# A four-layer graph network on one core: the fallback branch put last, layer 0's update set around the last far sums, and the products d and s in slot tiles of their own

## The chip, the core and the metric

The kernel runs on one core of a Trainium2 chip, in one launch. The metric is device microseconds of the whole program. All times are in microseconds (us) unless another unit is named.

The core has five engines that work side by side, each in the order of its own queue: TensorE (PE; its weight loads are listed as PEld), VectorE (DVE), ScalarE (ACT), GpSimd (POOL) and SyncE (SP), which here only issues transfers. They wait for each other by semaphores. SBUF is the working memory; PSUM holds what TensorE writes, in banks of 512 f32 per partition.

## What is computed

2708 nodes with 128 features `x`, and a dense matrix `adj` in which some 2.4% of the entries are not zero (with weights). Four layers follow each other, each as `x = layernorm(x + layer(x, adj))`. The change touches layer 0 and the way the layers hang together:

```python
s = x @ msg_w[:, :128].T
d = x @ msg_w[:, 128:].T
messages = gelu(s[:, None, :] + d[None, :, :] + msg_b)     # one vector for each pair i, j
aggregated = einsum('ijd,ij->id', messages, adj)
h = gelu(concat([x, aggregated]) @ upd_w.T + upd_b) + x
x = layernorm(x + layernorm(h) * ln_w + ln_b)
```

Layer 1 is a gated attention: queries and keys from `x`, `sigmoid(q k^T)` times `adj` twice, a product with the messages, an update and a layernorm. Layer 2 is a hyperbolic attention over the same pairs. Layer 3 is two products with `adj`, each followed by a matrix and a swish. Layers 1 to 3 keep their computation and their order.

## The kernel before

**Tiles.** The nodes are taken in NT = 22 tiles of 128 (the last has 20 rows), as columns in NB = 22 blocks of JB = 124, and as rows i of layer 0 in LT = 22 tiles of LR = 125 (NC = 5 groups of RG = 25). `groups()` gives the tiles of an update in seven groups: five of four tiles, one of one, and the last with 20 rows. `runs()` gives two halves of 11 tiles.

**Layer 0** computes the gelu only for pairs with an edge. In a block (one row tile by one column block) TensorE picks, for each row and each column of the block, the slots of the first few edges: ten matmuls `pick` (L716) of a selection S with `dA`, which holds d and the adjacency, each as two f16 parts (hi and lo) whose sum is the f32 value, once for each of the five groups; then L721 adds s. ScalarE takes the gelu of the slots (L760), VectorE weighs them (L747), and TensorE adds them up (L732, `add_up`). Edges beyond the slots of a block are "far": VectorE takes the largest of them by weight for each row (up to 16, in two rounds of 8), L676 finds their place, SP loads the row's s into `far` (`start_far`, far<-s_tab), POOL fetches and adds the rows of d with eight indirect transfers (L680), ScalarE takes their gelu (L686), and VectorE sums them (L694). `turn` and `close` (L700 to L706) add far and near sums and put them, transposed, into `aggT`. The three slot tiles `sl_all` (two PSUM banks each) are used in turn by the blocks.

The order of layer 0 is written out by hand (`tc.manual_schedule()`): every step has a block number at which it is issued (`when()`, `preparation()`), and the loop over the 484 blocks issues block by block the pick, the gelu, the weighing of the block before, and the steps that are due. Steps of the last rows with a number above 484 are issued after the loop.

**The preparation** is the part of these steps with negative numbers. `turn_x` transposes x on TensorE (L423) into the slot tiles, two groups of four tiles in the two banks of a tile, and DVE or ACT copies (L425). Then six `Piece`s of four tiles each come. `products` computes d (L449) in bank 0 of a slot tile and s (L460) in bank 1 of the same tile; DVE copies d (L453), ACT writes the hi part five times, once for a group (L455, 2560 elements), DVE adds the bias to s (L462), ACT takes s's hi part (L464), SP stores both to DRAM tables. `update` computes `x @ upd_w[:128] + upd_b` into u_tab (L478, L480). `rests` gives the lo parts on DVE (L488, L490), and POOL copies d's lo part to the four other groups (L492). Between these steps lie the first rows' own: masks (L579), ranks (L587, L588, L628), edges past the slots (L638 to L645), adjacency parts.

**After the loop** the count of rows that the sparse way cannot do, `bad_n`, is summed (L777 to L785: six small VectorE operations, one matmul, one cast), then the far steps of the last row tile are issued. SP loads u_tab into `new` (L791). All engines load `bad_n` (L793) and compare (L794): if it is above 0, layer 0 is done densely (it is 0 for these inputs, so the branch jumps over it). Then the update: for each group the product of `aggT` (L851) is added to `new` (L852), a gelu, x is added (L854), moments (L173). POOL computes `xb = x + ln_b` for all tiles in one instruction (L846). `resnorm` does two layernorms by halves: first half add, second half add, first half end, second half end. A layernorm's small values are chains of short VectorE operations with a square root on ScalarE; its scaling is one operation for a tile, on VectorE (L194) and ScalarE (L192) together.

**Layer 1** starts with transposes of two weights (L880, copied at L882) and of x (L892), and gives messages, keys and queries by groups (L895 to L899). POOL adds the bias row to x (L901) and then loads three broadcast vectors for layer 2 (`y_vecs`, L264); VectorE multiplies them at L270. SP loads rows of `adjT` ahead, three for layer 1 (L911) and four for layer 2 (L1122).

Of the kernel before, what the change touches and what calls it, by code (L numbers as in the profile page):

```python
# [11 lines left out]
F32 = mybir.dt.float32  # L12
BF16 = mybir.dt.bfloat16
# [6 lines left out]
P = 128  # L20
# [18 lines left out]
def gnn_stack(ctx: ExitStack, tc: tile.TileContext, t, out: bass.AP):  # L39
# [13 lines left out]

    def weight(name, k0=0):
        w = const.tile([P, D], F32, name=f"w_{name}_{k0}")
        nc.sync.dma_start(out=w, in_=t[name][k0:k0 + P, :])
        return w

    def column(name):
        c = const.tile([P, 1], F32, name=f"col_{name}")  # L60
        nc.sync.dma_start(out=c, in_=t[name].rearrange("(p o) -> p o", o=1))
        return c

    def across(name):
        n = t[name].shape[0]
        r = const.tile([P, n], F32, name=f"row_{name}")
        nc.gpsimd.dma_start(out=r, in_=t[name].partition_broadcast(P))
        return r
# [4 lines left out]
    nc.vector.memset(x[:, NT - 1, :], 0.0)  # L73
    if NFULL:
        nc.sync.dma_start(out=x[:, :NFULL, :], in_=t["x"][:NFULL * P, :].rearrange("(n p) d -> p n d", p=P))
    if NFULL < NT:
        nc.sync.dma_start(out=x[:rows[-1], NT - 1, :], in_=t["x"][NFULL * P:, :])
# [14 lines left out]
    class Values:  # L92
# [5 lines left out]
        def new(self, like=None):  # L98
            self.n += 1
            shape = [P, NT] if like is None else list(like.shape)  # L100
            return self.pool.tile(shape, F32, name=f"{self.tag}{self.n}")

# [93 lines left out]
    def resnorm(h, xb, g, st, V, sq=None):  # L196

        st2 = V.pool.tile([P, NT, 6], F32, name=f"{V.tag}_st2")
        for a, b in runs():
            normalize(h, h, st, a, b, V)  # L200
            nc.vector.tensor_tensor(h[:, a:b, :], h[:, a:b, :], over_tiles(g, b - a), op=ALU.mult)
            nc.vector.tensor_tensor(x[:, a:b, :], xb[:, a:b, :], h[:, a:b, :], op=ALU.add)
            moments(st2, x, a, b)
        for a, b in runs():
            normalize(x, x, st2, a, b, V, sq)
# [119 lines left out]
    with ExitStack() as l0:  # L325
# [6 lines left out]
        bad_n = wp.tile([1, 1], mybir.dt.int32, name="bad_n")  # L332
# [4 lines left out]
        with ExitStack() as msg:  # L337
# [80 lines left out]
            def turn_x():  # L418
                for n, (a, b) in enumerate(spans(0, NT, 4)):
                    ps = sl_all[n // 2][:, n % 2, :]  # L420
# [6 lines left out]
            class Piece:  # L427
# [7 lines left out]
                def products(self):  # L435
                    b0, b1, a0, a1 = self.b0, self.b1, self.a0, self.a1
                    ps = sl_all[(self.n + 1) % 3].rearrange("p k (b d) -> p k b d", d=D)
# [9 lines left out]
                    for b in range(b0, b1):  # L447
                        r = min(JB, N - b * JB)
                        nc.tensor.matmul(ps[:r, 0, b - b0, :], xT[:, b * JB:b * JB + r], msg_d, start=True, stop=True)  # L449
                        if r < JB:  # L450
                            nc.vector.tensor_copy(d[:r, b - b0, :], ps[:r, 0, b - b0, :])
                    full = min(b1, NFB) - b0
                    nc.vector.tensor_copy(d[:, :full, :], ps[:JB, 0, :full, :])  # L453
                    self.hi, self.lo = (v[:, b0:b1, :, :D] for v in dA)
                    nc.scalar.activation(self.hi, d[:, :, None, :].to_broadcast([JB, b1 - b0, NC, D]), AF.Copy,  # L455
                                         scale=D_SCALE)
                    for a, b, r in groups():
                        if a0 <= a < a1:
                            for i in range(a, b):
                                nc.tensor.matmul(ps[:r, 1, i - a0, :], xT[:, i * P:i * P + r], msg_s,  # L460
                                                 start=True, stop=True)
                            nc.vector.tensor_tensor(s[:r, a - a0:b - a0, :], ps[:r, 1, a - a0:b - a0, :],  # L462
# [4 lines left out]
                    for p0, p1 in even(JB):  # L467
                        nc.sync.dma_start(out=rows_of_d[p0:p1, b0:b1, :], in_=d[p0:p1])

# [15 lines left out]
                def rests(self):  # L485
# [6 lines left out]
                    nc.gpsimd.tensor_copy(lo[:, :, 1:, :], lo[:, :, 0:1, :].to_broadcast([JB, b1 - b0, NC - 1, D]))  # L492
# [12 lines left out]
            class Rows:  # L505
# [125 lines left out]
                def past(self, m):  # L631
                    if m == 0:
                        self.o = op_.tile([P, NB, JB], F32, name="o")
# [105 lines left out]

            LAG = 3  # L740
            assert NC == 5 and NB % 2 == 0
            R = [Rows(i) for i in range(LT)]
            steps = sorted(((g, n, step) for n, (g, step) in enumerate(x for v in [preparation(), *(v.when() for v in R)] for x in v)),
                           key=lambda x: x[:2])
            with tc.manual_schedule():
# [27 lines left out]

                most = vp.tile([P, 1], F32, name="most")
# [12 lines left out]
                for _, _, step in steps:  # L787
                    step()

        new = l0.enter_context(tc.tile_pool(name="l0x", bufs=1, reuse_waits="tile")).tile([P, NT, D], F32, name="new")  # L790
        nc.sync.dma_start(out=new, in_=u_tab.rearrange("(n p) d -> p n d", p=P))  # L791

        n_bad = nc.values_load(bad_n[0:1, 0:1])  # L793
        with tc.If(n_bad > 0), ExitStack() as msg:  # L794
            mp = msg.enter_context(tc.tile_pool(name="all", bufs=1))
            ap_ = msg.enter_context(tc.tile_pool(name="adjrows", bufs=2))
            gp = msg.enter_context(tc.tile_pool(name="gelu", bufs=3))
            psum = msg.enter_context(tc.tile_pool(name="ps_l0", bufs=2, space=PSUM))
            pbc = msg.enter_context(tc.tile_pool(name="ps_bc", bufs=2, space=PSUM))

            sel = mp.tile([3 * RG, RG], BF16, name="sel")
            nc.vector.tensor_add(sel, ident[:3 * RG, 0:RG], ident[:3 * RG, RG:2 * RG])
            nc.vector.tensor_add(sel, sel, ident[:3 * RG, 2 * RG:3 * RG])

            xT = mp.tile([P, N], F32, name="xT")
            sT = mp.tile([P, N], F32, name="sT")
            dT = mp.tile([P, N], F32, name="dT")
            transposed(xT, x, psum)  # L810
            linear_T(sT, msg_s, xT, psum, bias=msg_b)
            linear_T(dT, msg_d, xT, psum)

            HALF_N = -(-N // 2)
            halves = spans(0, N, HALF_N)
            part = mp.tile([P, N, len(halves)], F32, name="part")
            for g0 in range(0, N, RG):
                r0 = min(g0, N - RG)
                a = ap_.tile([3 * RG, N], F32, name="a")
                for k in range(3):  # L820
                    nc.sync.dma_start(out=a[k * RG:(k + 1) * RG, :], in_=adj[r0:r0 + RG, :])
                s = ap_.tile([3 * RG, N], BF16, name="s")
                nc.gpsimd.tensor_copy(s, a)
                for n in (2 * RG, RG):
                    nc.gpsimd.tensor_tensor(a[:n, :], a[:n, :], s[:n, :], op=ALU.subtract)
                    nc.gpsimd.tensor_copy(s[:n, :], a[:n, :])
                for i in range(g0, min(g0 + RG, N)):
                    one = sel[:, i - r0:i - r0 + 1].to_broadcast([3 * RG, P])
                    g = gp.tile([P, N], F32, name="g")
                    nc.scalar.activation(g, dT, AF.Gelu, bias=sT[:, i:i + 1])  # L830
                    for h, (b0, b1) in enumerate(halves):
                        bc = pbc.tile([P, HALF_N], F32, name="bc")
                        for c0, c1 in spans(b0, b1, BANK):
                            nc.tensor.matmul(bc[:, c0 - b0:c1 - b0], one, s[:, c0:c1], start=True, stop=True)
                        nc.vector.scalar_tensor_tensor(
                            g[:, b0:b1], g[:, b0:b1], 1.0, bc[:, :b1 - b0], op0=ALU.mult, op1=ALU.mult,
                            accum_out=part[:, i, h:h + 1])
            nc.vector.tensor_add(aggT[:, :N], part[:, :, 0], part[:, :, 1])

        with ExitStack() as upd:  # L840
            rp = upd.enter_context(tc.tile_pool(name="upd", bufs=1))
            psum = upd.enter_context(tc.tile_pool(name="ps_upd", bufs=4, space=PSUM))
            V = Values(rp, "v0_")
            xb = rp.tile([P, NT, D], F32, name="xb")
            st = rp.tile([P, NT, 6], F32, name="st")
            nc.gpsimd.tensor_tensor(xb, x, over_tiles(ln_b), op=ALU.add)  # L846
            for a, b, r in groups():
                g = new[:r, a:b, :]
                ps = psum.tile([P, BANK // D, D], F32, name="ps")
                for i in range(a, b):  # L850
                    nc.tensor.matmul(ps[:r, i - a, :], aggT[:, i * P:i * P + r], upd_a, start=True, stop=True)  # L851
                nc.vector.tensor_tensor(g, g, ps[:r, :b - a, :], op=ALU.add)  # L852
                nc.scalar.activation(g, g, AF.Gelu)
                nc.vector.tensor_tensor(g, g, x[:r, a:b, :], op=ALU.add)  # L854
                moments(st, new, a, b)
            resnorm(new, xb, ln_w, st, V)


# [663 lines left out]
```

## Time and profile before

| | |
|---|---|
| median of 3 runs | 2005.69 (2005.01 to 2007.13) |
| profiled execution | 2005.42 |
| its span | 2003.7 (1.7 lie around it) |
| mean granted TensorE clock | 0.918 |
| busy: PE, DVE, ACT, POOL | 1675.0, 1517.8, 1105.9, 666.0 |
| first pick (L716) | at 67.04 |
| last add-up of layer 0 ends | at 894.2 |
| x of layer 0 finished | at 953.54 |
| last output write issued, end of span | 2000.25, 2003.7 |

A line of the timeline has the start, the length, the engine, the line and operation, what is written and read, and in brackets how long the engine had been idle before and what released it. SPq, DVEq and ACTq are the sequencers of the engines: transfers issued, branches and register loads. A line of waits has who waited for whom, the sum, how often and the longest.

### The profile page before, as it was taken

What the parts mean: (1) busy time and instruction counts of PE and PEld (TensorE: products, weight loads), DVE (VectorE), ACT (ScalarE), POOL (GpSimd) and SP (SyncE); (2) the same over time, 40 slices, a digit from 0 to 9 for tenths busy, and PEclk for the clock granted to TensorE, in tenths of its full rate; (3) what the DMA queues carried; (4) which work ended last, traced back from release to release, by engine and by line L of the source; (5) the groups of instructions that cost most, each with busy time, mean ns of one, the idle gap of its engine ahead of it and who ended that gap; (6) DMA issues with size and microseconds to landing.
All of it is one profiled execution on the core that took longest, in us unless ns stands there. A gap on an engine that the chain in (4) does not pass through costs nothing. (4 is left out here: it accounts for less than half of the span.)

```text
span 2003.7 us, 36396 instructions
## 1 busy us (share of the span) xinstructions
PE 1675.0 (84%) x14037; PEld 959.1 (48%) x14037; DVE 1517.8 (76%) x3507; ACT 1105.9 (55%) x1510; POOL 666.0 (33%) x417
## 2 busy tenths in 40 slices
PE   5799999999999999871899994689999974079996
PEld 5566666666666666651444433423222322034543
DVE  5899999999999999857556567889999997820105
ACT  3567667666666676642333331599998993300103
POOL 2467767757767667461100000012000350000000
PEclk8899999999999999995899996779998987579998
DMA  7666666666667666343133310022222215135230
GB/s 178 155 139 131 133 136 140 126 136 148 124 133 148 130 129 139 73 85 143 36 135 136 142 60 0 1 87 87 75 80 94 80 42 245 46 115 187 107 127 28
DMA packets 218358, 222.25 MB, mean 111 GB/s; under 512 B 28372, under 2 KB 204474, under 8 KB 211714
## 3 DMA queue, kind: packets, MB, share of 16 engines
q1 hardware_dynamic: 167038, 195.95, 32.2%
q0 software_dynamic: 51136, 23.88, 10.3%
q8 instruction: 112, 1.84, 0.4%
q14 instruction: 72, 0.59, 0.1%
HBM read 211.94 MB, written 7.83 MB: 110 GB/s over the span
## 5 line engine op out<-in xcount | busy, mean ns | idle before, releaser
L680 POOL DMA_INDIRECT far<-d_tab,ix x352 | 563.0, 1599 | 257.5 <-DVE W L747 110.7
L760 ACT ACTIVATE g<-sl 128x768 f32<-128x768 f32 x484 | 393.0, 812 | 255.9 <-PE sl L721 199.1
L716 PE MATMUL sl<-dA,S 124*128 124x153 f16 x4840 | 408.0, 231 | 10.1 <-DVE W L747 7.7
L716 PEld LDWEIGHTS <-S 124*128 124x128 f16 x4840 | 330.4, 98 | 79.7 <-issue 67.9
L732 PE MATMUL acc<-g,W 128*32 128x128 f32 x4840 | 205.5, 277 | 0.7 <-DVE ones L777 0.7
L1125 POOL TENSOR_TENSOR at<-at,off 128x128 f32<-128x128 f32 (+1 forms) x22 | 68.1, 3113 | 338.1 <-DMA at<-in_adjT 320.4
L1441 PE MATMUL acc<-held,x 128*128 128x512 f32 (+1 forms) x240 | 99.6, 563 | 84.0 <-DVE x L194 84.0
L732 PEld LDWEIGHTS acc<-g,W 128*32 128x32 f32 x4840 | 140.6, 109 | 58.9 <-issue 54.7
L721 PE MATMUL sl<-s,same 50*128 50x384 f16 x968 | 161.9, 308 | 0.0
L233 DVE TENSOR_TENSOR g<-ps,row_L_gnn_b 128x512 f32<-128x512 f32 (+2 forms) x14 | 7.9, 572 | 197.1 <-PE ps L231 197.0
L923 ACT ACTIVATE w<-lg,row_L_gnn_gate_bias 128x512 f32<-128x512 f32 (+1 forms) x132 | 80.7, 634 | 137.8 <-PE lg L922 74.3
L1181 PE MATMUL accV<-m,X 128*128 128x512 f32 (+4 forms) x264 | 128.4, 628 | 33.6 <-DVE m L1171 29.2
L747 DVE TENSOR_TENSOR W<-sl,own 128x150 f32<-128x150 f32 x484 | 143.0, 299 | 14.6 <-ACT g L760 14.1
L1133 PE MATMUL ps<-XT 128*128 128x512 f32 (+4 forms) x264 | 143.2, 626 | 3.1 <-ACT m L1138 2.8
L676 DVE FIND_INDEX8 ix<-v,o 128x8 uint32<-128x2728 f32 x44 | 131.7, 2993 | 0.0
L607 DVE TENSOR_SCALAR S<-rk 124x1000 f16<-124x1000 bf16 (+1 forms) x330 | 129.4, 418 | 0.0
L922 PE MATMUL lg<-qT,mT 128*128 128x512 f32 (+2 forms) x264 | 115.5, 567 | 13.5 <-ACT w L923 9.9
L925 DVE TENSOR_TENSOR w<-w,at 128x2708 f32<-128x2708 f32 (+1 forms) x22 | 65.4, 2974 | 79.3 <-ACT w L923 79.3
L694 DVE SCALAR_TENSOR_TENSOR extra<-far,v,extra 128x128 f32<-128x128 f32 x330 | 114.4, 347 | 12.3 <-ACT far L686 6.0
L1441 PE MATMUL acc<-at,x 128*128 128x512 f32 (+3 forms) x288 | 116.7, 552 | 0.0
L638 DVE SCALAR_TENSOR_TENSOR o<-ps,ar 128x496 f32<-128x496 f32 x132 | 82.4, 624 | 38.3 <-issue 22.6
L1400 ACT COPY nT<-acc 128x512 f32<-128x512 f32 (+1 forms) x12 | 6.4, 530 | 186.7 <-PE acc L1441 186.7
(310 smaller groups left out, 2687.1 us busy)
## 6 DMA issues: line engine op xcount, KB each, us to landing
at<-in_adjT SPq DMA_DIRECT2D x40, 1354.0 KB
ar<-in_adj SPq DMA_DIRECT2D x105, 248.0 KB
far<-s_tab SPq DMA_DIRECT2D x44, 512.0 KB
at<-in_adjT SPq DMA_DIRECT2D x42, 448.0 KB
at<-in_adjT SPq DMA_DIRECT2D x21, 704.0 KB
at<-in_adjT SPq DMA_DIRECT2D x21, 650.0 KB
held<-in_adjT SPq DMA_DIRECT2D x10, 1354.0 KB
at<-in_adjT SPq DMA_DIRECT2D x21, 280.0 KB
```

The source lines that it names most:

```text
L607: nc.vector.tensor_scalar(self.S[h][:, :n, :, k * RG:(k + 1) * RG], self.rk[h][:, :n, :LR].rearrange("p b (c i) -> p b c i", c=NC), EDGE + ...
L676: nc.vector.max_index(ix, self.v[:, n * 8:n * 8 + 8], self.o.rearrange("p b j -> p (b j)"))
L680: nc.gpsimd.indirect_dma_start(out=self.far[n][:, k, :], out_offset=None, in_=d_tab[:, :], in_offset=bass.IndirectOffsetOnAxis(ap=self.ix[ ...
L716: nc.tensor.matmul(group[c], self.S[h][:, n, c, :], dA[q][:, b, c, :], start=c % 3 == 0 and q == 0, stop=False)
L721: nc.tensor.matmul(out, same[p], self.s3[p, :e - a, :], start=False, stop=True)
L732: nc.tensor.matmul(self.acc[q:q + 32, k, :], W[:, c, :], g[:, c, :], start=b == 0 and k == 0, stop=ends)
L747: nc.vector.tensor_tensor(W[:, :, :RG].rearrange("p (k c) i -> p k c i", k=2), columns_of(sl, D, DA), own[:, None, None, :].to_broadcast([ ...
L760: nc.scalar.activation(g.rearrange("p (k c) d -> p k c d", k=2), columns_of(sl, 0, D), AF.Gelu, scale=1.0 / D_SCALE)
L922: nc.tensor.matmul(lg[:r, :b - a], mT[:, j * P:j * P + r], qT[:, a:b], start=True, stop=True)
L1133: nc.tensor.matmul(ps, XT[:, self.js], XT[:, c], start=True, stop=False)
L1181: nc.tensor.matmul(accV[:, a:b], X[:self.r, self.j, :], self.m[:, a:b], start=first, stop=last)
L1441: nc.tensor.matmul(acc[k], src[:rows[j], j, :], at[:rows[j], a:b], start=j == order[0], stop=j == order[-1])
```

## The change

Three things are changed.

*The branch.* `n_bad` is read and compared at the end of the whole kernel and no longer between the sums and the update of layer 0. Layers 1 to 3 become a function. If `n_bad` is above 0, x is loaded again, layer 0 is done densely with its own update, and layers 1 to 3 are run once more. To the program that adds a second copy of these layers that is not run. The weights' loads are cached, so that the second copy uses the same tiles.

*The update.* It moves into the hand-written order. u_tab is loaded as a step of the last row tile, into the buffer `o` in which the edges past the slots were searched, and so ahead of the last load of far<-s_tab. The update of the first five groups (20 tiles, whose sums are closed before) is issued around the last far gelu and the last far sums; the half of the first 11 tiles is added next, then come groups 5 and 6, the other half, and the two ends. `ln_b` is added to x in place, a group at a time, on POOL. Small values lie in slots of the `g` pool, products in the slot tiles. The check of bad rows (seven operations, as before) comes behind all this.

*The pieces.* d and s get bank 0 of two different slot tiles. The copy of d is ACT's. ACT writes d's hi part once (512 elements) and POOL spreads it to the four other groups, as it did for the lo part. `turn_x` takes the slot tiles in the order 0, 1, 2.

```diff
             def turn_x():
-                    ps = sl_all[n // 2][:, n % 2, :]
+                    ps = sl_all[n % 3][:, n // 3, :]
...
                 def products(self):
-                    ps = sl_all[(self.n + 1) % 3].rearrange("p k (b d) -> p k b d", d=D)
+                    psd, pss = (sl_all[(2 * self.n + k) % 3][:, 0, :].rearrange("p (b d) -> p b d", d=D)
+                                for k in range(2))
...
-                    nc.vector.tensor_copy(d[:, :full, :], ps[:JB, 0, :full, :])
+                    nc.scalar.copy(d[:, :full, :], psd[:JB, :full, :])
...
-                    nc.scalar.activation(self.hi, d[:, :, None, :].to_broadcast([JB, b1 - b0, NC, D]), AF.Copy,
-                                         scale=D_SCALE)
+                    nc.scalar.activation(self.hi[:, :, 0, :], d, AF.Copy, scale=D_SCALE)
+                    self.spread(self.hi)
...
+                def spread(self, v):
+                    nc.gpsimd.tensor_copy(v[:, :, 1:, :], v[:, :, 0:1, :].to_broadcast(
+                        [JB, self.b1 - self.b0, NC - 1, D]))
...
+            class Update:
+                def when(self):
+                    yield (LT - 1) * NB + 7, self.load
+                def load(self):
+                    o = op_.tile([P, max(NB * JB, NT * D)], F32, name="o")
+                    self.new = o[:, :NT * D].rearrange("p (n d) -> p n d", d=D)
+                    nc.sync.dma_start(out=self.new, in_=u_tab.rearrange("(n p) d -> p n d", p=P))
...
+                def sums(self, n):
+                    a, b, r = groups()[n]
+                    g, ps = self.new[:r, a:b, :], sl_all[n % 3][:r, n // 3 % 2, :].rearrange("p (i d) -> p i d", d=D)
+                    for i in range(a, b):
+                        nc.tensor.matmul(ps[:, i - a, :], aggT[:, i * P:i * P + r], upd_a, start=True, stop=True)
+                    nc.vector.tensor_tensor(g, g, ps[:, :b - a, :], op=ALU.add)
+                    nc.scalar.activation(g, g, AF.Gelu)
+                def rows(self, n):
+                    a, b, r = groups()[n]
+                    g = self.new[:r, a:b, :]
+                    nc.vector.tensor_tensor(g, g, x[:r, a:b, :], op=ALU.add)
+                    moments(self.st, self.new, a, b)
+                    nc.gpsimd.tensor_tensor(x[:r, a:b, :], x[:r, a:b, :], over_tiles(ln_b, b - a, r), op=ALU.add)
...
                 R[-1].add_up(late)
+                rest = [step for _, _, step in steps]
+                last_gelu, far_sums, last_turn = rest[0], rest[1:9], rest[9:]
+                G = len(groups())
+                ahead = LR * (LT - 1) // BANK
+                U.open()
+                for n in range(ahead):
+                    U.sums(n)
+                    if n > 0:
+                        U.rows(n - 1)
+                    if n == 1:
+                        last_gelu()
+                    if n == 2:
+                        for step in far_sums:
+                            step()
+                for step in last_turn:
+                    step()
+                U.rows(ahead - 1)
+                early, late = runs()
+                U.norm.add(*early)
+                for n in range(ahead, G):
+                    U.sums(n)
+                for n in range(ahead, G):
+                    U.rows(n)
+                U.norm.add(*late)
+                U.norm.end(*early)
+                U.norm.end(*late)
...
-                for _, _, step in steps:
-                    step()
...
+    with ExitStack() as top:
+        layers_1_to_3(top)
+    n_bad = nc.values_load(bad_n[0:1, 0:1])
+    with tc.If(n_bad > 0), ExitStack() as top:
+        load_x()
+        all_pairs()
+        layers_1_to_3(top)
```

## What is predicted

> **What bounds the kernel now.** I began with engines by stretch. The first row is the preparation of layer 0 (from the end of the transposes of x to the first pick, L716), the second its 484 blocks, the third all from the last add-up to the finished x. The columns are length, busy time and instructions of each engine, granted clock, DMA share, GB/s.
>
> ```profile
> core 0: us, PE busy (x) PEld busy (x) DVE busy (x) ACT busy (x) POOL busy (x), PEclk, DMA share, GB/s
> 18.30:67.00 48.70, 31.07 (x157) 27.03 (x157) 31.35 (x67) 21.64 (x21) 10.51 (x5) 0.77 0.72 179
> 67.00:894.20 827.20, 781.50 (x11368) 561.00 (x11366) 761.26 (x2170) 554.11 (x823) 563.99 (x353) 1.00 0.63 128
> 894.20:953.70 59.50, 10.15 (x54) 9.21 (x54) 38.86 (x158) 13.44 (x32) 6.14 (x2) 0.59 0.40 146
> ```
>
> The loop is TensorE's: 94% busy, 1.71 us a block. The change does not touch it, so what the stretches around it gain or lose is the result. Both are chains of waits: no engine is busy for more than two thirds of either. Next the waits of the preparation (who waited for whom, us in total, times, longest):
>
> ```profile
> POOL dA L492 <- DVE dA L490: 42.1, 5, 15.1
> ACT dA L455 <- DVE g L453: 21.9, 6, 6.6
> PE sl L460 <- DVE g L453: 11.6, 6, 3.6
> PE sl L423 <- DVE aggT L425: 2.4, 3, 0.8
> ```
>
> PE loses 11.6 us before the s products, because VectorE's copy of d reads the tile they write, and 2.4 us in the transposes. POOL is idle for most of the stretch. The timeline shows one such piece and the neighbour of a POOL copy:
>
> ```profile
> 36.42 0.68 DVE L453 COPY g<-sl 124x512 f32<-124x512 f32 x1
> 37.14 2.35 ACT L455 ACTIVATE dA<-g 124x2560 f16<-124x2560 f32 x1 [4.58 <-DVE g L453]
> 37.16 2.08 PE L460 MATMUL sl<-w_L_msg_wT,aggT 128*128 128x128 f32 x8 [1.18 <-DVE g L453]
> ...
> 51.94 2.03 POOL L492 COPY dA<-dA 124x2048 f16<-124x2048 f16 x1 [5.68 <-DVE dA L490]
> 53.48 0.91 DVE L579 TENSOR_SCALAR mask<-at 124x768 bf16<-124x768 f32 x1
> ```
>
> Last the timeline behind the loop, down to layer 1's first query copy:
>
> ```profile
> 892.13 0.71 SPq L791 DMA_DIRECT2D new<-u_tab  x1
> ...
> 901.37 1.06 ACT L686 ACTIVATE far<-far 128x1024 f32<-128x1024 f32 x1 [6.52 <-issue]
> 902.46 3.06 DVE L694 SCALAR_TENSOR_TENSOR extra<-far,v,extra 128x128 f32<-128x128 f32 x8 [6.02 <-ACT far L686]
> ...
> 907.50 0.26 ACT L706 COPY aggT<-ps 128x125 f32<-128x125 f32 x1 [5.08 <-PE ps L703]
> 910.71 0.29 PEld L851 LDWEIGHTS ps<-w_L_upd_wT,aggT 128*128 128x128 f32 x1 [3.38 <-ACTq L794]
> 910.73 3.01 SPq L911 DMA_DIRECT2D at<-in_adjT  x3
> ```
> ```profile
> 965.02 0.56 DVE L270 TENSOR_TENSOR y_prods<-y_vecs 128x384 f32<-128x384 f32 x1 [3.76 <-DMA y_vecs<-in_L_gnn_att_wr]
> 965.50 0.68 DVE L899 COPY qT<-ps_q 128x512 f32<-128x512 f32 x1
> ```
>
> VectorE does nothing useful from 894 to 902.5 while the last fetched rows land, then all wait for the turn and the branch (16 us from 894.2 to 910.7), and only then does the update start, although 20 of 22 tiles' sums were closed long before. At the end VectorE stands 3.76 us at L270 for y_vecs, ahead of the query copy that layer 1 waits for.
>
> **Preparation: −8 us, between −11 and −4.** Own banks for d and s take away the 11.6 us; three transposed groups that need no copy first take 2.4: at most 14.0 on PE. VectorE loses L453, 6 × 0.68 + 0.5 = 4.6 us. ScalarE takes these copies (7, about 0.6 each, +3.7) and its L455 falls from 2.35 to 0.63 (a 512-element copy, as L464): 6 × −1.72 = −10.3. I walked the list in order, each instruction starting when its engine and its producers are free, at the trace's durations: PE leaves the transposes at 16.1 instead of 18.3, and the first pick comes at 57.6 instead of 67.04, −9.4. The other 4.6 of the 14.0 come back as waits for the ranks' chain (L588, L640), to which PE now comes sooner. The same bytes (48.7 us × 179 GB/s = 8.7 MB) in 39.3 us are 222 GB/s, a share of 0.89: not yet full on average, but 24.6 to 34 us is at 0.99 already, so an engine may wait for a load there. Against it stand six new POOL copies like L492 (2.0 us, the last 1.05), 11 us in POOL's idle time; the last is due only when block 20 is picked. If that cover were gone, the next piece would come up to 2 us late.
>
> What they cost VectorE is open. By the row, L579's mask of 768 took 0.91 us beside L492 and 0.54 at 846.7 with no copy beside it: 0.37 an overlap, some four of six on VectorE's path, 1.5 us. The Trainium skill ("SBUF — State Buffer", Who interferes with whom) has a harder rule, against this change: VectorE and GpSimd share a port pair as an exclusive lock, and the loser stands for the whole instruction: up to 11 us. The row shows a slow-down of a third of a microsecond, no stand of 2, so I take 1.5: −9.4 + 1.5 = −7.9. Ends: −11 (more than the walk, if the ranks' waits do not all return) and −4 (nearly three full stands of 2).
>
> **Layer 0's end: x finished 9.3 us sooner, −5 at layer 1, between −9.3 and −1.3.** In the old clock: the last add-up ends at 894.2, the first group's sum at 895.5. Five groups at 2.34 (L852 0.69, residual 0.67, statistics 0.87 and a gap) and 3.2 of far sums are 14.9: VectorE is through at 910.7. Then the early half's add: value chain 4.0 with its Sqrt table load of 1.28, 2.2 for the scaling (8 × 0.27), 1.62 twice, statistics 2.22: 922.4. Groups 5 and 6 add 2: 924.5. The late half's add 10.2, the two ends 4.8 and 4.6: 944.2, against 953.54. The far sums, the turn and the 2.6 us of branch now lie beside VectorE's other work; the old 6.12 us row addition on POOL (L846) becomes seven pieces under the same cover. The second table load (Gelu back, 1.28) is hidden by VectorE's queue.
>
> Two orders are moved on SP. The u_tab load goes from 892.1 to where the `o` tile comes free (the last FIND_INDEX8, L676, ends at 867.6) and stands ahead of the last far<-s_tab load. It takes DMA 8 us by its old landing, the s_tab load about 4: 880, and POOL needs that at 879.7: 0 to 2 us, inside the 6.5 us that the last gelu waited. In return, it no longer delays the last fetch. Second, layer 1's first loads (L911) waited for nothing after 910.7; now their tile is free only after the check of the bad rows, which stands behind the update (six small operations and a cast, 1.7 us, before hidden at 895): 945.4. They and the four of layer 2 are 7.0 MB and took 17 us at 400 GB/s and more, so they end about 963.7.
>
> That is where the gain is cut. Layer 1's transposes start 6.1 us earlier (948.6 for 954.76; the check and the transposes of its weights come between), and the first query product is there at 956. But ahead of its copy VectorE waits at L270. POOL issues y_vecs behind its own 6.13 us addition, at 950.6 to 952.3. In the trace they landed 3.3 us later with DMA empty: 955.6, and the gain stays 9.3. Now they land among the 7.0 MB. The nearest row is the start: a broadcast row issued at 2.36 beside the load of x landed at 10.70, 8.3 later. The Trainium skill ("DMA: Bandwidth & Descriptors", Queues, rings and completion order) says an engine goes round its queues packet by packet, which would put y_vecs ahead of most of the 7.0 MB: some 955.6 to 958. The row, with its 8.3, gives 960. I take the row, as it holds the same kind of transfer beside the same kind of load: the copy moves from 965.5 to about 960.5, −5. The bounds are 9.3 (no contention) and 1.3 (they end with the loads at 963.7).
>
> **Branch at the end: +1.7, between +0.8 and +4.** The load of the count (0.48) and the branch stand behind everything. ScalarE's took 2.6 us (908.0 to 910.6), VectorE's 2.9, POOL's 4.3 beside a full DMA. The last output write is issued at 2000.3 and lands at 2002.8, 2.5 us that hide most of it on the engines that are done at 2000.0: 0.5 + 2.9 − 2.5 = 0.9, and if SP branches only after its write, 3.4. I take 1.7. Without the cover it is 3.4.
>
> Sum, against the profiled execution (2005.42, its span 2003.7 and 1.7 around it): −7.9 − 5 + 1.7 = −11.2, so 1994.2; that execution is 0.3 below the median of 2005.69, the same by any measure here.
>
> **Rivals.** *The preparation's gain is eaten by DMA*: its stretch is at 0.99 from 24.6 to 34 and a shorter one asks for more; then only turn_x's 2 us stay, −2 − 5 + 1.7 = −5.3: 2000. For it: the share; against it: PE's waits name VectorE, not DMA. *y_vecs end with the loads*: −7.9 − 1.3 + 1.7 = −7.5: 1998. *y_vecs pass them*: −7.9 − 9.3 + 1.7 = −15.5: 1990. *The port lock, slower*: each of the twelve POOL copies of the preparation holds VectorE for its whole 2 us, the six new ones on the path of the piece. They cost 11 us plus what the earlier pieces now run into; that decides from 9.4 + 5 − 1.7 = 12.7 us, 2.1 a copy. With 2.7 a copy and the branch at +4, the time is 2005.4 − 9.4 − 5 + 16 + 4 = 2011. The 0.91 of L579 speaks against it. *It does not overlap as it says*: the update's second gelu stands behind the last far gelu on ScalarE in order, and if the fetch lands as late as 901.4, VectorE stops until then: the start is lost by up to 5 us, and the time is 1998, not more, as nothing else of the update waits for it.
>
> **Chances.** Forecast (1991 to 1997.5) 0.45; y_vecs pass or the walk is exceeded (1985 to 1991) 0.18; y_vecs with the loads, the late gelu or DMA in the preparation (1997.5 to 2001.7) 0.23; several of them together, no change to be told 0.09; the lock, slower 0.05. A measurement of this kernel tells about 0.2%, 4 us, from none: faster 0.86, same 0.09, slower 0.05. The range is 1986 to 2001.5.
>
> **What would show it.** First pick at 57 to 61; no PE wait for a copy at the s products; operations of VectorE beside POOL copies longer by about 0.4, not 2; the last far gelu before 899 less the shift; x finished about 17 before its old 953.5; a wait of some 4 us at the y_vecs products with the first loads of layer 1 in flight; behind the last output write 1 to 2 us of branch. The forecast is wrong if the first pick stays near 65, if layer 1 begins less than 10 us sooner, or if the loop's 827 us change.

## The result, and the profile after

The changed kernel takes 1994.97 us (median of 5 runs, 1993.64 to 1996.88) against 2005.84 of the kernel before in the same session: ratio 0.9943, 95% interval 0.9933 to 0.9954. The forecast was 1994.2. The number was met; two of its three terms were not, and it was luck that their errors cancel. The profiled executions show it, stage by stage (1993.64 with a span of 1991.8, against 2005.42 and 2003.7):

| stage, by its marks in the two traces | before | after | difference | forecast |
|---|---|---|---|---|
| start to first pick | 67.04 | 53.08 | −14.0 | −7.9 |
| first pick to the last add-up's end | 827.15 | 827.46 | +0.3 | 0 |
| from there to x of layer 0 | 59.35 | 49.82 | −9.5 | −9.3 |
| from x to the first query copy | 11.96 | 17.55 | +5.6 | +4.3 |
| from there to the issue of the last output write | 1034.75 | 1035.16 | +0.4 | 0 |
| from there to the end of the span | 3.45 | 8.73 | +5.3 | +1.7 |
| sum | 2003.7 | 1991.8 | −11.9 | −11.2 |

Engines by stretch after the change, in the columns of the prediction's first fence: preparation (from the end of the transposes), loop, update.

```profile
core 0: us, PE busy (x) PEld busy (x) DVE busy (x) ACT busy (x) POOL busy (x), PEclk, DMA share, GB/s
14.50:53.08 38.58, 22.48 (x157) 19.59 (x157) 34.14 (x61) 16.04 (x30) 20.66 (x11) 0.84 0.91 239
53.08:880.50 827.42, 782.88 (x11369) 561.96 (x11367) 762.26 (x2169) 554.38 (x823) 563.27 (x354) 0.99 0.64 130
880.50:930.40 49.90, 7.91 (x52) 6.69 (x50) 43.50 (x154) 15.89 (x34) 7.55 (x8) 0.57 0.02 2
```

Two things in the first row were not in the prediction. TensorE does the same 157 matmuls in 22.5 us and no longer 31.1. And VectorE is busy 34.1 us, 2.8 more than before, although it has six instructions fewer: 88% of the stretch, so it is the busiest engine now. The waits of that time (who waited for whom, us in total, times, longest):

```profile
POOL dA L508 <- DVE dA L531: 18.8, 6, 5.0
...
ACT g L489 <- PE sl L484: 10.5, 5, 4.8
...
PE ps L669 <- DVE count L682: 8.8, 3, 3.6
```

TensorE's 11.6 us at the s products are gone; what it waits for now is VectorE's work on the first rows (L682, the old L640). The fourth piece in the timeline shows both surprises:

```profile
33.33 1.06 PE L486 MATMUL sl<-w_L_msg_wT,aggT 128*128 128x128 f32 x8
...
34.23 3.96 POOL L508 COPY dA<-dA 124x2048 f16<-124x2048 f16 x2 [3.31 <-DVE dA L531]
...
34.42 0.69 DVE L498 TENSOR_TENSOR far<-sl,row_L_gnn_msg_b 128x512 f32<-128x512 f32 x1 [0.25 <-PE sl L486]
34.45 1.11 PE L519 MATMUL acc<-w_L_upd_wT,aggT 128*128 128x128 f32 x8
...
35.03 3.46 DVE L648 TENSOR_SCALAR S<-rk 124x1000 f16<-124x1000 bf16 x2
```

The eight matmuls of s take 1.06, where the same piece had 2.07 before. (The third piece, which the prediction's fence shows with 2.08, still takes 1.91.) And two selections (L648) take 3.46 between them, 0.76 before. The first copy ends at 36.14 and the first selection at 36.44; the second copy ends at 38.20 and the second selection at 38.49. So each stands until the copy beside it is through. Not every operation of VectorE does: L498, which reads PSUM, begins inside the first copy and takes its usual 0.69.

Behind the loop, down to layer 1's first query copy:

```profile
883.82 1.04 ACT L728 ACTIVATE far<-far 128x1024 f32<-128x1024 f32 x1
...
886.77 3.44 DVE L736 SCALAR_TENSOR_TENSOR extra<-far,v,extra 128x128 f32<-128x128 f32 x8
...
893.48 0.25 ACT L748 COPY aggT<-ps 128x125 f32<-128x125 f32 x1
...
931.47 1.31 SPq L1013 DMA_DIRECT2D at<-in_adjT  x3
...
937.56 0.62 POOL L299 DMA_DIRECT2D y_vecs<-in_L_gnn_b  x1
...
947.44 0.56 DVE L305 TENSOR_TENSOR y_prods<-y_vecs 128x384 f32<-128x384 f32 x1 [7.80 <-DMA y_vecs<-in_L_gnn_att_wr]
947.91 0.68 DVE L1001 COPY qT<-ps_q 128x512 f32<-128x512 f32 x1
```

The last far gelu waits for nothing (3.3 us behind the last add-up; before 7.2), the turn lies beside the update, and x is complete at 930.4. Then VectorE stands 7.8 us for y_vecs instead of 3.8. At the kernel's end, the last output write and the branch (instructions, count, shortest/median/longest in ns, first and last start):

```profile
1983.07 0.97 SPq L1576 DMA_DIRECT2D out<-x  x1
```
```profile
L1601 SPq EVENT_SEMAPHORE  x8: 17/17/17, 1987.8 to 1990.1; - x8
...
L1601 SPq COMPARE_BRANCH  x1: 54/54/54, 1984.8 to 1984.8; - x1
L1601 ACTq EVENT_SEMAPHORE  x1: 17/17/17, 1985.0 to 1985.0; - x1
L1601 DVEq EVENT_SEMAPHORE  x1: 21/21/21, 1985.2 to 1985.2; - x1
```

SP is the last: it issues until 1984.0, loads the count (0.7), compares at 1984.8, is at the branch's target at 1987.8, and its eight semaphores there take until 1990.1. ScalarE and VectorE are through by 1985.2. Of the 2.3 us at the target, 1.7 are one gap between the fourth semaphore and the fifth, which no view here explains. The output itself is not what is late: the last packet of the last write is through at 1985.0.

### The profile page after: what moved, and what is told of

Read it like the earlier page. It is cut to its first block, busy times and chain, and to the rows that moved or that the text cites. A ratio compares the mean times of both kernels' runs of the same rounds, so it can differ in the third digit from the quotient of the medians.

```text
span 1991.8 us, 36394 instructions
## 1 busy us (share of the span) xinstructions
PE 1663.9 (84%) x14037; PEld 949.8 (48%) x14037; DVE 1526.7 (77%) x3500; ACT 1103.2 (55%) x1519; POOL 679.0 (34%) x429
## 5 line engine op out<-in xcount | busy, mean ns | idle before, releaser
L648 DVE TENSOR_SCALAR S<-rk 124x1000 f16<-124x1000 bf16 (+1 forms) x330 | 134.0, 431 | 0.0
L1024 PE MATMUL lg<-qT,mT 128*128 128x512 f32 (+2 forms) x264 | 115.6, 567 | 18.6 <-ACT w L1025 9.9
L680 DVE SCALAR_TENSOR_TENSOR o<-ps,ar 128x496 f32<-128x496 f32 x132 | 82.4, 624 | 37.3 <-PE ps L669 30.0
```

Source lines behind the costliest of these rows:

```text
L648: nc.vector.tensor_scalar(self.S[h][:, :n, :, k * RG:(k + 1) * RG], self.rk[h][:, :n, :LR].rearrange("p b (c i) -> p b c i", c=NC), EDGE + ...
L1024: nc.tensor.matmul(lg[:r, :b - a], mT[:, j * P:j * P + r], qT[:, a:b], start=True, stop=True)
```

## The experiments

A time is compared by its ratio to the kernel before on the same chip. To separate what is smaller than that interval, the first pick's time in the trace is given too; the six kernels with the whole of the changed preparation had it at 52.7 to 55.2, and the stretch from the first query copy to the last output write takes 1032.9 to 1036.1 in the kernels that change nothing in it, so single traces tell no less than some 3 us.

**The third part alone.** The kernel before with the pieces and transposes of the change (the part of the diff in `turn_x` and `Piece`), nothing else.

> The kernel before with the third part of the change only: d and s in slot tiles of their own, ACT's copy of d, the hi part spread by POOL, the new order of the transposes. Branch and update stay as they were. Theory A (from the trace after, where the first pick comes 14.0 us sooner, at 53.1 for 67.0, and the loop is as long as before): the preparation alone gives -14, about 1991.8. Rival B (the prediction's term, -8, and something else brought the first pick forward, for instance a load that landed sooner by chance): about 1997.8. By A the matmul groups of eight in the preparation take 1.05 us and no longer 2.0 in most pieces, and VectorE has single operations of 2 us beside POOL's copies.

1992.36; ratio 0.9935 (0.9921 to 0.9948), first pick at 52.65. Theory A: the preparation alone brings at least the whole gain (1.6 us more than the full change by the ratios, which is inside the intervals). VectorE's long operations are there too, under other line numbers: two selections take 3.80 together, and the operation that is L529 in the changed kernel takes 2.19 once.

**The third part undone.** The changed kernel with the pieces and transposes of before.

> The changed kernel with the third part undone: transposes and pieces as before, the update around the far sums and the branch at the end stay. Theory A (the stages add: x of layer 0 9.5 us sooner against the loop's end, 5.6 of it given back at y_vecs, 5.3 to 6 lost at the end): slower than the kernel before by 1 to 3 us, about 2008. Rival B (the prediction's terms -5 and +1.7): faster by 3.3, about 2002.5.

2008.46 over 21 runs; ratio 1.0010 (1.0003 to 1.0016). Theory A, in the middle of its 1 to 3: the update around the far sums and the branch at the end together make the kernel slower by about 2 us. The stages in its trace: update 49.84, from x to the query copy 17.24, behind the last write 8.42. What the first takes off (9.5), the other two give back (5.3 and 5.0).

**Without the branch.**

```diff
-    n_bad = nc.values_load(bad_n[0:1, 0:1])
-    with tc.If(n_bad > 0), ExitStack() as top:
-        load_x()
-        all_pairs()
-        layers_1_to_3(top)
```

> The changed kernel without the read of the count of bad rows and the branch at its end: this leaves out the dense fallback, which these inputs do not need. Theory A (from the trace after: the last output write is issued at 983.1 past 1000 and the span ends 8.7 us later, where before it was 3.45): the branch at the end costs 5.3 us, so about 1989.7. Rival B (the prediction's term): it costs 1.7, so about 1993.3, and the long tail belongs to something else, such as a late write. By A the span ends some 3.4 us behind the last issue.

1988.69; ratio 0.9916 (0.9902 to 0.9929). Its last write and its span's end (1988.8) are 3.5 apart, as in the kernel before:

```profile
1985.28 0.45 SPq L1576 DMA_DIRECT2D out<-x  x1
```

Theory A: the branch costs 5.2 us in the trace (8.73 against 3.5), and the tail is the branch's.

**The last writes by ScalarE.**

```diff
+                q = nc.scalar if b == NT else nc.sync
                 if a < m:
-                    nc.sync.dma_start(out=out[a * P:m * P, :]...
+                    q.dma_start(out=out[a * P:m * P, :]...
```

> The changed kernel with the last two output writes issued by ScalarE and no longer by SP. Theory A (from the trace after: the end is set by SP alone, which issues the last write until 984.0, loads the count for 0.7, branches for 3.0 and then needs 2.3 for eight semaphores, while ScalarE and VectorE are through at 985.2): SP branches ahead of the end, ScalarE's branch takes 2.9 behind its write, and 2 to 3 us are gained: about 1992.5. Rival B (the tail is the landing of the write and the end of the program behind the branch, whoever issues): within 0.7 of the changed kernel, 1995.

1989.80; ratio 0.9921 (0.9907 to 0.9935). SP now branches beside the last normalize, ScalarE's branch is the last:

```profile
L1602 SPq COMPARE_BRANCH  x1: 54/54/54, 1973.8 to 1973.8; - x1
...
L1602 ACTq COMPARE_BRANCH  x1: 54/54/54, 1982.7 to 1982.7; - x1
...
L1602 ACTq EVENT_SEMAPHORE  x1: 17/17/17, 1985.2 to 1985.2; - x1
```

The write is issued at 1981.18 and the span ends at 1986.2: 5.0 and no longer 8.7. Theory A; its 2 to 3 us were 3.7 in the trace. What is left on ScalarE is 0.8 for the load of the count and 2.5 for the branch; the tail is 1.5 longer than without a branch.

**The branch ahead of layer 1**, with y_vecs early (the next experiment's edit).

```diff
+    n_bad = nc.values_load(bad_n[0:1, 0:1])
+    with tc.If(n_bad > 0):
+        load_x()
+        all_pairs()
     with ExitStack() as top:
         layers_1_to_3(top)
```

> The changed kernel with y_vecs issued at the head of layer 1 as in the run before (which took 1987.0), and the branch put between layer 0's update and layer 1: the dense way would give x there, and layers 1 to 3 stand once in the program. Theory A: a branch costs what the last engine needs for it, 0.5 + 2.9 to 3.8 ahead of layer 1, and y_vecs and the loads of adjT are issued as much later; the tail's 5 to 6 us are gained back: 1 to 2 us faster than the run it comes from, about 1985.5. Rival B: SP and POOL need 5 us and more for it beside each other's instruction loads, y_vecs are waited for again, and the place is no better or worse than the end: 1987 to 1991.

1991.67; ratio 0.9931 (0.9918 to 0.9945), against 0.9909 (0.9894 to 0.9924) with the branch at the end. Theory A fell; B holds, at the upper end of its 1987 to 1991 and a little beyond. All engines load the count at 933.3 to 933.6 and reach the target only at 938.4 to 939.4:

```profile
L1597 ACTq COMPARE_BRANCH  x1: 50/50/50, 933.8 to 933.8; - x1
...
L1597 PEldq COMPARE_BRANCH  x1: 5286/5286/5286, 933.9 to 933.9; - x1
...
L1597 ACTq EVENT_SEMAPHORE  x1: 17/17/17, 939.1 to 939.1; - x1
```

Five engines that branch at once need 4.3 to 5.5 us for it. In the changed kernel it is 2.8 and 2.9 for ScalarE and VectorE, which come to it together, and for engines that come to it alone 3.0 (SP), 3.6 (TensorE) and 4.0 (GpSimd). Whether it is the meeting of the five that costs more is not shown: here a load of adjT, issued at 933.2 ahead of the branch, keeps the DMA engines 78% busy from 935 to 937. In the kernel before, SP and GpSimd alone branched at 897.0 beside a full DMA, and needed 5.0 and 4.3. Between x and the first query copy lie 6.7 us more than with the branch at the end (18.7 for 12.0), and the tail is 4.9 shorter (3.7 for 8.6).

**y_vecs at the head of layer 1.**

```diff
+            weights2 = Weights2(wp)
+            weights2.load()
             with ExitStack() as pre:
...
-                    if j == NT // 4:
-                        weights2.load()
```

> The changed kernel with one order changed: the three broadcast rows y_vecs (and the three columns beside them) are issued at the head of layer 1, ahead of POOL's addition of the bias row (6.1 us) and of the three loads of adjT on SP. Theory A: VectorE's wait of 7.8 us for y_vecs ahead of the first query copy is what cut the gain of the earlier update; it goes, the copy stands at about 940 for 947.9, and the time falls by 6 to 8, to about 1988. Rival B: what is late next is the first rows of adjT (7 MB, landing until about 951) or TensorE's half clock, and less than 3 us are gained: 1992 or more.

1987.03; ratio 0.9909 (0.9894 to 0.9924). Theory A. The query copy comes 12.0 us behind x and no longer 17.6:

```profile
940.85 1.04 DVE L305 TENSOR_TENSOR y_prods<-y_vecs 128x384 f32<-128x384 f32 x1 [5.20 <-DMA y_vecs<-in_L_gnn_att_wr]
```

The wait shrinks, it does not go: the last of the rows is issued at 934.74 and there at 940.85, 6.1 later, although the loads of adjT stand behind them: only 0.2 of their 7.0 MB had moved by 940. What held the rows is open; POOL's own addition (L1006) runs beside them from 935.3 to 941.5.

**The hi part by ScalarE again.**

```diff
-                    nc.scalar.activation(self.hi[:, :, 0, :], d, AF.Copy, scale=D_SCALE)
-                    self.spread(self.hi)
+                    nc.scalar.activation(self.hi, d[:, :, None, :].to_broadcast([JB, b1 - b0, NC, D]), AF.Copy,
+                                         scale=D_SCALE)
```

> The changed kernel with d's hi part written to all five groups by ScalarE again (one operation of 2560 elements a piece, 2.35 us), without POOL's six extra copies; own slot tiles and ACT's copy of d stay. Theory A: VectorE bounds the shortened preparation (34.1 of 38.6 us busy), and about 7 us of that are operations that stand still beside POOL's copies (2.15 and 2.18 us for 0.43 and 0.69); with half of the copies gone, 3 to 5 us come back: about 1991. Rival B: ScalarE's 10 us more delay the copies of d and the casts of the ranks that TensorE waits for, and the preparation gets longer by 2 to 4 us: about 1998. No change would say that the lock falls where VectorE waits anyway.

1990.20; ratio 0.9923 (0.9909 to 0.9936), first pick at 50.49. Groups of operations up to the first pick, first in the changed kernel, then here (busy, mean ns of one):

```profile
L648 DVE TENSOR_SCALAR S<-rk 124x1000 f16<-124x1000 bf16 x10 | 7.6, 805 | 0.0
L529 DVE SCALAR_TENSOR_TENSOR far<-far 128x512 f16<-128x512 f32 x5 | 5.6, 1121 | 0.0
```
```profile
L648 DVE TENSOR_SCALAR S<-rk 124x1000 f16<-124x1000 bf16 x10 | 3.8, 422 | 0.0
...
L529 DVE SCALAR_TENSOR_TENSOR far<-far 128x512 f16<-128x512 f32 x5 | 3.4, 684 | 1.0 <-ACT far L500 1.0
```

The six extra copies cost VectorE 6.0 us in these two lines alone, and the first pick 2.6. Theory A, with a gain of uncertain size: 2.6 in the trace, about 4 by the ratios, whose intervals still touch. That it is a gain, two later kernels with the same edit confirm (the last two below): their first picks come at 52.3 and 51.7, and all three lie ahead of the six with POOL's copies (52.7 to 55.2), by 2.3 in the mean. So this one part of the change is a loss.

**Own tiles undone**: `sl_all[(self.n + 1) % 3][:, k, :]` for d and s, the rest as changed.

> The changed kernel with d and s of a piece back in the two banks of one slot tile; ACT's copy of d, the spreading by POOL and the new transposes stay. Theory A (the slot tiles are what matters: s's products wait for the copy of d): most of the 14 us of the preparation is given back, 8 to 12, about 2003 to 2007, with waits of TensorE at the s products. Rival B (what mattered is that the copy left VectorE's queue: ScalarE is free and copies within about a microsecond of the d products): 2 to 4 us are given back, 1997 to 1999, six waits of about 0.8 us.

1997.53; ratio 0.9955 (0.9942 to 0.9969), first pick at 58.58. By time it is B: of the 14 us, 2 to 3 (5.5 at the first pick) belong to the tiles as such, and not the most of it, as the prediction had it. But not by its waits: the s products do not wait six times for ACT's copy; ScalarE waits 18.3 us for the s products before its copy of d, as the profile's waits say. They go to the same tile and are issued ahead of the copy, which so waits for them.

```profile
ACT g L489 <- PE sl L486: 18.3, 5, 6.6
```

**The old order of the transposes**: `sl_all[n // 2][:, n % 2, :]` in `turn_x`.

> The changed kernel with the transposes of x in the old order of banks, so that TensorE waits three times for a copy. Theory A: 2 to 4 of the 14 us belong to the transposes (they ended at 14.5 and no longer at 18.3), about 1998. Rival B: a later start is made up behind, since VectorE bounds the stretch: within 1.5 of the changed kernel.

1998.90; ratio 0.9966 (0.9953 to 0.9978), first pick at 59.71. Theory A, beyond its 2 to 4: 4.6 us are given back by the ratios and 6.6 at the first pick. The d products start at 18.6 and no longer at 14.5, and these 4.1 us are not made up behind.

**More matmuls in the pauses.** The kernel before, and in `products`, ahead of the s products:

```diff
+                    for i in range(4):
+                        nc.tensor.matmul(sl_all[(self.n + 2) % 3][:, 1, :P], xT[:, i * P:(i + 1) * P], msg_d,
+                                         start=True, stop=True)
```

> The kernel before with four matmuls more in each of the six pieces, between the d and the s products, where TensorE waits 1.2 to 3.8 us for VectorE's copy; their result is not read. Theory A (part of the 14 us is the granted clock: TensorE's groups of eight took 2.0 us in most pieces before and 1.05 after, 31.1 us busy against 22.5 for the same work, and pauses are what lowers the clock): with fewer pauses the groups take 1.05 in more of the pieces, and the first pick comes 1 to 4 us sooner in spite of more work, about 2003. Rival B: the clock does not follow from pauses of this length; the extra work costs 1 to 6 us, 2007 to 2012, and groups take 2.0 as before.

2002.28 over 12 runs; ratio 0.9984 (0.9975 to 0.9993), faster with more work. The median matmul of the d products took 421 ns in the kernel before and takes 273 here, as in the changed kernel, and so do those of s and of the update (421 to 275):

```profile
L449 PE MATMUL sl<-w_L_msg_wT,aggT x44: 270/273/575, 18.4 to 58.2; 128*124 128x128 f32 x42, 128*104 128x128 f32 x2
```

That is A for the clock: shorter pauses keep it up. The matmuls that were there before are busy for some 8 us less, and the added ones for 8.9. But the first pick comes only 1.0 us sooner (66.0); of the 3.7 us by which this trace is shorter, the stretch from the last add-up to x has 2.6 (56.7 for 59.35), and nothing was changed there. So the clock's effect is shown in the durations, not its size in the time; B's extra cost did not come either.

**Three edits together**: hi by ScalarE, y_vecs early, last writes by ScalarE.

> The changed kernel with three edits together: the hi part by ScalarE (4.8 gained alone), y_vecs at the head of layer 1 (8.0 gained alone), the last writes issued by ScalarE (2.5 expected alone). They lie in three stages with the TensorE-bound loop between them. Theory A: their gains add, -15 against the changed kernel, about 1980. Rival B: the hi part's gain is not clear of noise alone (its first pick came only 2.6 us sooner in the trace), so -12 to -13, about 1982.5.

1983.02; ratio 0.9883 (0.9868 to 0.9898), nearer to B. This is 12 us better than the changed kernel.

**The same with y_vecs on SP's queue** (`nc.sync` for `nc.gpsimd` in `Weights2.load`).

> The three edits together (1983.0 in the run before), with y_vecs issued on SP's queue and no longer on POOL's. Theory A: y_vecs on POOL's queue landed 5.5 us behind their last issue even ahead of the loads of adjT, since both queues are served in turns; on SP's queue they stand in front of these loads and land in 3 to 4, VectorE's wait of 5.2 shrinks to 2 to 3, and 2 to 3 us are gained: about 1980.5. Rival B: the landing is the descriptors' own (three rows to 128 partitions, 512 bytes each), whoever issues, and what is won is lost to the later issue of adjT: 1982 to 1984.

1983.03; ratio 0.9884 (0.9869 to 0.9899). By time it is B: the two are not told apart. Its trace shows the landing that A said: the rows are there 3.8 us after the last is issued (932.9), where it was 8.3 in the run before, and the query copy comes 10.5 us behind x, where it was 13.7 there and 12.0 with y_vecs early alone. The medians show nothing of it. A's reason, that the loads of adjT are served in turn with the rows, could explain the 8.3, since there the first of these loads was issued ahead of the last row. It does not explain the 6.1 with y_vecs early alone, where the loads had hardly begun.

```profile
936.65 0.56 DVE L305 TENSOR_TENSOR y_prods<-y_vecs 128x384 f32<-128x384 f32 x1 [3.88 <-DMA y_vecs<-in_L_gnn_att_wr]
```

## Why the prediction was right, and where it was not

**The preparation, −7.9 with bounds at −11 and −4: mis-sized, and outside its bounds.** Its step "at the trace's durations" failed. The walk gave the groups of eight matmuls their lengths of before, mostly 1.9 to 2.1 us; once the pauses were shorter, 11 of the 15 groups of d, s and the update took 1.14 or less, and TensorE's busy time fell by 8.6 us. The long groups lie where the granted clock is half. Two stretches of the trace of before, in the columns of the first fence: the first holds a d group of 1.04 us (at 42.32), the second an s group of 2.07 (at 44.94).

```profile
41.10:44.30 3.20, 1.40 (x11) 1.03 (x8) 3.02 (x5) 1.53 (x3) 0.00 (x0) 1.00 0.66 167
44.50:51.10 6.60, 6.16 (x32) 5.95 (x32) 4.43 (x11) 2.99 (x2) 1.75 (x1) 0.50 0.79 194
```

That durations depend on the waits around them was a missing term, and the 0.77 in the prediction's own first row was its sign. The Trainium skill ("TensorE: Matmul & The Clock Gate", What's actually happening) has the rule: the array runs at half clock by default, and a window of about 3.4 us of activity decides on the next. The trace's clock agrees: from 27.3 on, where its record begins, it is 1.0 or 0.5 and changes in steps of 3.4 us. How much of the missing 6 us it makes is not shown, since more matmuls shortened the durations and left the first pick nearly where it was. Two more terms of the walk were off. The transposes were left at 14.5 and not at 16.1. And the 11.6 us were put down to the tiles of d and s; with one tile again only 2.4 (5.5 at the first pick) came back, so at least half of them goes with other parts, such as the copy's move to ScalarE, which was never undone alone.

The second failing step has the other sign: "The row shows a slow-down of a third of a microsecond, no stand of 2, so I take 1.5." The row was misread. L579 began at 53.48, and the POOL copy beside it ended at 53.97, 0.49 later; L579 ended at 54.39, 0.4 behind the copy. It had stood for all that was left of the copy, which is the lock of the rule that was set aside. L648 (2.15 us for 0.43) and L529 (2.18 for 0.69) show it in full: they too end 0.3 and 0.5 behind a copy, each a little less than its own time.

```profile
20.16 4.17 POOL L508 COPY dA<-dA 124x2048 f16<-124x2048 f16 x2 [1.21 <-DVE dA L531]
...
22.68 2.18 DVE L529 SCALAR_TENSOR_TENSOR far<-far 128x512 f16<-128x512 f32 x1
```

The price was 6.0 us on VectorE and some 2.6 at the first pick, not 1.5. The rival that built on the lock was right in its mechanism and wrong in its size: not every copy meets an operation, and not every operation that meets one stands. The section of the Trainium skill that the prediction cites ("SBUF — State Buffer", Who interferes with whom) has this limit, which the prediction left out: an operation of VectorE with at most one input in SBUF, outside the modes that use two ports, does not contend with GpSimd. The trace agrees for L498 and L680, which take one of their inputs from PSUM and keep their 0.69 and 0.65 beside a copy.

**Layer 0's end: right.** −9.5 for −9.3, by the steps as they were put: the far sums take 3.4 us of VectorE, forecast 3.2, and the turn and the gelu of the last rows lie beside the update. The load of u_tab ahead of far<-s_tab held nothing up; the last far gelu came 3.3 us behind the last add-up, 7.2 before. The rival of a late gelu did not happen.

**y_vecs: right, by the row.** The copy of the queries moved from 965.5 to 947.9, or 3.9 sooner in the old clock, forecast 5. Issued last at 938.7, the rows were there at 947.44, 8.7 later; the start's row had 8.3. The 955.6 to 958 that the prediction drew from the rule of going round the queues did not come: it was 961.1 in the old clock. But the rule itself is not refuted. The rows' packets ran from 941.3 to 946.8 beside the loads, and at 947.4 only 4.2 of the 7.0 MB had landed; the loads went on until 955.1. So the rows passed a part of the loads, and needed 5.6 us between their first and last packet, where they needed 3.4 alone in the kernel before. Issuing the rows at the head of layer 1 gave 7 us.

**The branch, +1.7 with bounds at +0.8 and +4: mis-sized, outside its bounds.** The step "2.5 us that hide most of it" failed. SP takes one thing after another and issues last, so it branches only behind its write; the prediction named this case with 3.4, and took 1.7 between it and 0.9. And its way is not 0.5 + 2.9 but 0.7 + 3.0 + 2.3, with the eight semaphores at the target. The cover was shorter too: the last packet of the old write was through at 2002.1, not 2002.8. The trace of before had SP's branch too, 5.0 us from 897.0 on beside a full DMA; the prediction's list has ScalarE's, VectorE's and POOL's and leaves it out. Two experiments confirm it: without the branch the tail is 3.5, and with another engine issuing last it is 5.0.

**The sum** was right within 1 us by luck: −6.1 for the preparation and +3.6 for the branch cancelled in part, and +1.3 at y_vecs and smaller terms took most of the rest. What the forecast said of the change as a whole is therefore no more than half true: the third part alone gave −14.0, and the first two, forecast at −3.3, gave +2.

What stays open: why the kernel with more matmuls gained 3.2 us by the ratio and 1.0 at the first pick; how the 14 us divide between the clock, the transposes, the tiles and ScalarE's copy; the size of the gain with the hi part on ScalarE, which the ratios put near 4 us and the first picks near 2.5; and what delays the rows of y_vecs, and a branch beside a load.

## What to carry to other kernels

Where the granted clock of a stage is well below 1 (0.77 here), its matmuls have two lengths (421 ns and 273), and they can shrink when waits go: cost such a change from both. When an operation beside a GpSimd copy looks only a little longer, compare its end with the copy's end before calling the contention small. A branch cost each engine here 2.5 to 4.1 us behind its last instruction, and up to 5.5 beside a load; the engine that issues the last output pays it last, so the output is better issued by one that gets through the branch sooner (tail 5.0 us with ScalarE, 8.7 with SP).

## What the runs showed of the hardware

- The branch at the kernel's end took 2.5 to 4.1 us on an engine. Ahead of layer 1, where five came together with a load under way, it took 4.3 to 5.5; in the kernel before, on two beside a full DMA, 4.3 and 5.0.
- Three broadcast rows of 64 KB landed 8.7 us after the last was issued beside 7 MB of loads; 6.1 and 8.3 on POOL's queue ahead of these loads in the program, 3.8 on SP's queue.
- More matmuls in TensorE's pauses made the matmuls around them shorter (medians of 421 ns to 273).
- Beside a GpSimd copy, VectorE's selections (L648) and its lo parts of s (L529) stood until the copy's end and ended 0.3 to 0.5 us behind it; operations that read PSUM (L498, 0.69) and MAX8 (L687, 0.4) kept their length.
